# Flamingo block on one Trainium2 core: the recurrence of the fourth batch element, moved 4.8 places along the order of work

## The chip, the cores and the metric

The kernel runs on one core of a Trainium2 chip. The metric is the device time of one execution in microseconds (us), as the median of several runs. The engines are named as in the profile: PE is TensorE (matrix products and transposes; PEld is its weight load), DVE is VectorE, ACT is ScalarE, POOL is GpSimd, and SP issues nearly all DMAs. Each engine, and SP's queue, works through its own list of instructions in a fixed order.

## The reference

Four batch elements x[b] of 512 tokens by 512 channels pass through two layers, each an attention-like part and an FFN, all with residual sums and a gate (the tanh of a scalar):

```python
x = x + tanh(g_xattn[0]) * wkv(w, u, k=layernorm(x), v=ctx)          # "WKV"
x = x + tanh(g_ffn[0])   * ffn0(layernorm(x), w1, w2, w3)            # "FFN"
x = x + tanh(g_xattn[1]) * attention(layernorm(x), ctx, wq, wkv, wp) # "attention"
x = x + tanh(g_ffn[1])   * ffn1(layernorm(x), gamma, W)              # "ternary layer"
```

- **WKV** is a recurrence along the 512 tokens for every channel: a running maximum o, and two running sums p and q with decays; y = (A p + E v) / (A q + E), where A and E are exponentials of differences to the running maximum.
- **ffn0** is w3 of silu(w1 x) * (w2 x), with 2048 hidden channels, weights reduced to their sign times a mean, and activations rounded to 8 bits in groups of 64.
- **attention** has 16 heads of 32 channels; queries come from x (rounded to 8 bits), keys and values from the context ctx.
- **ffn1** normalises by the root mean square, rounds to 8 bits and multiplies with a weight matrix of -1, 0 and 1 times a scale.

The elements ("batch 0" to "batch 3" below, and their FFN stages by the same number) don't depend on one another. Inside one element the four parts follow each other.

## The kernel before

**Tiling.** Tokens are cut in NT = 4 tiles of 128, channels in NC = 4 chunks of 128, the FFN's hidden channels in NF = 4 quarters of 512. The first layer's FFN of one element has 16 *units*, one for each (token tile, quarter). A unit has two matrix products of 8 matmuls each (`up`, into the PSUM tile `ff_hp`; activations are split in two parts for precision), tanh on ACT (`gate`, L745), two products on DVE (L746, L750), rounding (`quantised`, L670-688, DVE, ACT, and POOL at L685), four transposes and a split (`parts`, L697 on DVE) and 8 matmuls into `ff_acc` (`down`).

**WKV of one element** is `wkv_layer(b, xb)`, from L562. It has three phases:

1. Statistics (`layernorm`, L191 and L194 on DVE, two small steps on POOL).
2. For each of the four token tiles: the normalised rows `wk_xn` on ACT (L215), four transposes into the PSUM tile `wk_ps` on PE, a copy to `wk_k` on ACT (L584).
3. For each of the four channel chunks, the generator `chunk(c)`: a scan for the running maximum (L599, DVE), a difference (L608, POOL), four Relu (L612) and two Exp (L614) on ACT, a scan for q (L629, DVE), products on POOL (L630, L635, L636, L641, L642) and DVE (L632, L645), a scan for p (L634, DVE), two reciprocals over 256 columns (L640, DVE), four transposes back (`wy_ps`), and the update of xb (L653, DVE). For b > 1, the context chunk `wk_v` comes from DRAM by a DMA (L594). A chunk has ten steps, and a chunk starts eight steps after the one before it (`in_steps(chains, 8)`).

The tiles of WKV come from a pool with one buffer each (`wk_k`, `wk_e`, `wk_o`, `wk_p`, `wk_q`, and `wk_v`, whose buffer `wk_xn` shares), so two elements' WKV can't be in flight together in the same phase.

**The order of work.** Four elements are in flight at different parts. Every part is a Python generator that issues a few instructions per step. `line(gen, (start, end, steps), ...)` registers a generator with a *place* for each step, spread evenly from start to end. `run` always takes the step with the smallest place. A place's whole number is a batch element's FFN: places b to b + 1 hold the 16 units of element b and one more, SLOTS = 17 places of the grid each (element 0's stage, with the weights' preparation, runs by its own scale up to 0.99). Below, "slot n of stage b" is b + n/17. So in stage 2, for example, lie:

- the FFN of element 2: slots 0 to 17.75
- the attention of element 0: its main part up to slot 5.95, its output projection to 8.35 (`project_out`, L1036, L1037 and others), its ternary layer from 8.95 to 13.95 (`ternary`: `tf_xn`, L219, L1147, L231, L1159, L1172)
- the attention of element 1: preparation at slots 1.7 to 4.35, the main part from 4.95 on (unit by unit: scores `s_ps`, maximum `at_nm` L948, Exp `at_P` L950, transposes `pt_ps` and copies `at_PT` L970, values `o_ps`)
- the WKV of element 3 (`next_batch(3)`)

Stage 1 holds the same for elements 1, 0 and 2, without the older element's tail, projection and ternary layer. Stage 3 holds the same as stage 2, one element on, without a WKV.

`next_batch(b)` is one step for the load of x[b] (L554), one for the statistics, four for the normalised rows and transposes (the last transposes come with the first chunk's step), and 32 for the chunks. This is the code that the change touches. On top of the issue order, the framework's scheduler decides the final place of each instruction on its engine, among those issued near it; so a step that is issued earlier stands earlier, but not by an exact count.

Of the kernel before, what the change touches and what calls it, by code (L numbers as in the profile page):

```python
# [30 lines left out]
def kernel(  # L31
# [1155 lines left out]
    def next_batch(b):  # L1187
        xs[b] = load_batch(b)
        yield
        yield from wkv_layer(b, xs[b])  # L1190
# [29 lines left out]
    SLOTS = NT * NF + 1  # L1220

    def line(gen, *parts, aside=False):
        lines.append({"gen": gen, "parts": parts, "step": 0, "aside": aside})

    xs = {}
    with (
# [19 lines left out]
        def at_unit(n):  # L1246
            return 0.3 + 0.67 * n / 16.0
# [84 lines left out]
            (at_unit(16), at_unit(16.4), 7),  # L1332
        )
        line(next_batch(1), (at_unit(0.5), at_unit(0.5), 1), (at_unit(0.6), at_unit(0.6), 1), (at_unit(2.0), at_unit(5.0), 4), (at_unit(5.0), at_unit(14.0), 32))
        for b in (2, 3):
            line(
                next_batch(b),
                (b - 1.0 - 4.2 / SLOTS, b - 1.0 - 4.2 / SLOTS, 1),
                (b - 1.0 - 3.2 / SLOTS, b - 1.0 - 3.2 / SLOTS, 1),
                (b - 1.0 + 1.8 / SLOTS, b - 1.0 + 5.8 / SLOTS, 4),  # L1340
                (b - 1.0 + 5.05 / SLOTS, b - 1.0 + 13.05 / SLOTS, 32),
            )
        run(0.99)
    nc.sync.dma_start(out=gamma_b, in_=bcast(gamma))
# [79 lines left out]
```

## Time and profile before

| what | value |
|---|---|
| runs | 1093.74, 1093.9, 1095.42 us; median 1093.9 us |
| the profiled execution | 1094.21 us; span of its instructions 1092.4 us, mean granted TensorE clock 0.956 |
| stage 1, first `ff_hp` product of unit 0 to that of stage 2 | 328.6 to 513.4 us |
| stage 2, the same way | 513.4 to 738.4 us |
| x[3] loaded by the DMA issued at | 279.4 us |
| WKV of element 3: statistics | 486.3 to 489.6 us (starts) |
| its copies to `wk_k` (L584) | 541.6, 555.7, 566.4, 570.5 us |
| its first scans (L599) | 571.2, 573.8, 605.2, 657.1 us |
| its updates of xb (L653) | 599.8, 636.7, 669.4, 697.0 us |
| statistics of element 3's FFN | 698.2 to 700.2 us (starts) |

A profile shows busy time of engines, and for each wait what ended it. Busy shares of the whole span are means over stages that differ; the windows (busy time of each engine in chosen stretches) show one stage at a time. [...]

### The profile page before, as it was taken

What the parts mean: (1) busy time and instruction counts of PE and PEld (TensorE: products, weight loads), DVE (VectorE), ACT (ScalarE), POOL (GpSimd) and SP (SyncE); (2) the same over time, 40 slices, a digit from 0 to 9 for tenths busy, and PEclk for the clock granted to TensorE, in tenths of its full rate; (3) what the DMA queues carried; (4) which work ended last, traced back from release to release, by engine and by line L of the source; (5) the groups of instructions that cost most, each with busy time, mean ns of one, the idle gap of its engine ahead of it and who ended that gap; (6) DMA issues with size and microseconds to landing.
All of it is one profiled execution on the core that took longest, in us unless ns stands there. A gap on an engine that the chain in (4) does not pass through costs nothing.

```text
span 1092.4 us, 17928 instructions
## 1 busy us (share of the span) xinstructions
PE 943.3 (86%) x6350; PEld 680.0 (62%) x6380; DVE 827.0 (76%) x1600; ACT 729.9 (67%) x1490; POOL 320.7 (29%) x328
## 2 busy tenths in 40 slices
PE   3879997998879888799997886999999999878975
PEld 2345564565557666677775665677776777655652
DVE  5985548757876899896769898966687866579976
ACT  5656755567545776667877576677685777877863
POOL 3831104423333254621215545412122410100000
PEclk8889999999999999999999798999999999989998
DMA  8188845464445674645576354655574563244311
GB/s 288 39 272 317 323 169 190 144 221 155 154 146 181 221 234 127 231 129 169 185 234 204 121 177 133 204 195 180 184 231 156 184 210 116 59 148 116 116 42 39
DMA packets 85674, 189.68 MB, mean 174 GB/s; under 512 B 12241, under 2 KB 36817, under 8 KB 74577
## 3 DMA queue, kind: packets, MB, share of 16 engines
q1 hardware_dynamic: 85584, 188.53, 51.7%
q8 instruction: 51, 0.84, 0.3%
q14 instruction: 39, 0.31, 0.1%
HBM read 148.65 MB, written 39.85 MB: 173 GB/s over the span
## 4 chain that ended last, share of the span: by engine, by line
PE 49%; DVE 22%; ACT 14%; POOL 5%; issue 5%; DMA 4%; SPq 1%; ACTq 0%; POOLq 0%; DVEq 0%
PE ff_hp L162 15%; PE pt_ps L165 7%; PE ff_acc L162 6%; PE o_ps L162 4%; PE v_ps L162 4%; PE s_ps L162 3%; ACT at_P L950 3%; DVE wk_q L640 3%; ACT at_PT L970 3%; DVE at_nm L948 2%; PE k_ps L162 2%; DVE wk_p L634 1%; PE qr_ps L165 1%; PE tp_ps L165 1%; ACT wk_e L612 1%
## 5 line engine op out<-in xcount | busy, mean ns | idle before, releaser
L162 PE MATMUL ff_hp<-wT,xp 128*128 128x512 f32 x1024 | 275.7, 412 | 6.6 <-DVE ff_z L746 3.7
L162 PEld LDWEIGHTS ff_hp<-wT,xp 128*128 128x128 f32 x1024 | 195.4, 196 | 54.6 <-DVE ff_z L746 5.7
L950 ACT ACTIVATE at_P<-s_ps,at_nm 128x512 f32<-128x512 f32 x256 | 175.0, 690 | 45.2 <-DVE at_nm L948 43.4
L948 DVE TENSOR_REDUCE at_nm<-s_ps 128x1 f32<-128x512 f32 x256 | 166.6, 677 | 38.4 <-PE s_ps L162 37.9
L970 ACT COPY at_PT<-pt_ps 128x512 f32<-128x512 f32 x224 | 131.2, 590 | 72.6 <-PE pt_ps L165 71.9
L685 POOL TENSOR_TENSOR ff_z<-qg_b,qg_s 128x512 f32<-128x512 bf16 x64 | 71.9, 1124 | 314.6 <-ACT qg_b L684 304.7
L165 PE MATMUL pt_ps<-ident,at_P 128*128 128x128 f32 x1024 | 155.4, 280 | 9.0 <-ACT at_PT L970 4.3
L165 PEld LDWEIGHTS pt_ps<-ident,at_P 128*128 128x128 f32 x1024 | 118.1, 142 | 47.3 <-ACT at_PT L970 10.9
L162 PE MATMUL ff_acc<-wT,hr 128*128 128x512 f32 x512 | 137.6, 409 | 5.2 <-DVE hr L697 2.6
L162 PE MATMUL s_ps<-at_kR,at_qR 128*128 128x512 f32 x256 | 103.0, 464 | 24.0 <-ACT at_P L950 17.6
L162 PEld LDWEIGHTS ff_acc<-wT,hr 128*128 128x128 f32 x512 | 92.9, 191 | 26.2 <-DVE hr L697 4.2
L162 PE MATMUL o_ps<-at_PT,at_V 128*32 128x128 f32 x2048 | 75.4, 281 | 4.7 <-ACT at_PT L970 2.8
L162 PEld LDWEIGHTS o_ps<-at_PT,at_V 128*32 128x32 f32 x2048 | 54.8, 111 | 28.6 <-issue 11.6
L746 DVE SCALAR_TENSOR_TENSOR ff_z<-ff_z,ff_hp 128x512 f32<-128x512 f32 x64 | 43.4, 679 | 37.0 <-ACT ff_z L745 36.9
L745 ACT ACTIVATE ff_z<-ff_hp,coef 128x512 f32<-128x512 f32 x64 | 44.1, 688 | 40.5 <-PE ff_hp L162 38.1
L750 DVE SCALAR_TENSOR_TENSOR ff_z<-ff_hp,coef,ff_z 128x512 f32<-128x512 f32 x64 | 47.7, 745 | 30.2 <-PE ff_hp L162 30.1
L684 ACT CAST qg_b<-qg_i 128x512 bf16<-128x512 int8 x80 | 49.3, 617 | 27.4 <-DVE qg_i L680 17.3
L162 PEld LDWEIGHTS s_ps<-at_kR,at_qR 128*128 128x128 f32 x256 | 43.3, 194 | 36.4 <-ACT at_P L950 25.2
L162 PE MATMUL v_ps<-wkvT,cT 128*128 128x512 f32 x128 | 60.5, 618 | 5.5 <-DVE wT L303 2.3
L162 PE MATMUL k_ps<-cT,wkvT 128*128 128x512 f32 x128 | 61.3, 631 | 2.3 <-ACT wk_k L584 1.0
L640 DVE RECIPROCAL wk_q<-wk_q 128x256 f32<-128x256 f32 x32 | 54.5, 1722 | 3.0 <-POOL wk_q L635 1.6
L696 ACT CAST hr<-tp_ps 128x512 fp32r<-128x512 f32 x64 | 37.6, 588 | 21.7 <-PE tp_ps L165 21.7
(180 smaller groups left out, 1669.4 us busy)
## 6 DMA issues: line engine op xcount, KB each, us to landing
wT<-wD SPq DMA_DIRECT2D x72, 1024.0 KB, 5.4
wn<-in_L_ffn_w_dram SPq DMA_DIRECT2D x18, 1024.0 KB, 6.2
at_kR<-kD SPq DMA_DIRECT2D x128, 128.0 KB, 4.0
at_qR<-qD SPq DMA_DIRECT2D x256, 64.0 KB, 2.5
wD<-wT SPq DMA_DIRECT2D x12, 1024.0 KB, 4.2
kD<-k_half SPq DMA_DIRECT2D x16, 512.0 KB, 2.8
qD<-at_half SPq DMA_DIRECT2D x32, 256.0 KB, 2.2
cn<-in_ctx_dram SPq DMA_DIRECT2D x8, 512.0 KB, 5.9
```

The costliest lines, as they stand in the source:

```text
L162: return in_turn(nc.tensor.matmul(*args, **kwargs))
L165: return in_turn(nc.tensor.transpose(*args))
L640: nc.vector.reciprocal(half, half)
L684: nc.scalar.copy(qb, qi)
L685: nc.gpsimd.tensor_tensor(grouped(src), grouped(qb), s.unsqueeze(2).to_broadcast([P, NG, GS]), ALU.mult)
L696: nc.scalar.copy(part[:, 0, :], pt)
L745: nc.scalar.activation(z, hp, AF.Tanh, scale=coef[:, 0:1])
L746: nc.vector.scalar_tensor_tensor(z, z, 1.0, hp, ALU.add, ALU.mult)
L750: nc.vector.scalar_tensor_tensor(z, hp, coef[:, 1:2], z, ALU.mult, ALU.mult)
L948: nc.vector.tensor_reduce(nm, sp, AX.X, ALU.max, negate=True)
L950: nc.scalar.activation(lanes[k, i, t], sp, AF.Exp, bias=nm, accum_out=sums[k][:, t, i : i + 1],)
L970: made[k] = nc.scalar.copy(dst, blocks(pt))
```

## The change

The registration of `next_batch(b)` for b = 2 and b = 3 is rewritten around a helper `slot(n)`, with a shift `first` that is 0 for element 2 and -4.8 slots for element 3.

| step | element 2 before | element 2 after | element 3 before | element 3 after |
|---|---|---|---|---|
| load | slot -4.2 of stage 1 | -4.2 | slot -4.2 of stage 2 | -9.0 |
| statistics | -3.2 | -2.8 | -3.2 | -7.4 |
| rows and transposes (4 steps) | 1.8 to 5.8 | 1.8 to 4.6 | 1.8 to 5.8 | -3.0 to -0.2 |
| chunks (32 steps) | 5.05 to 13.05 | 5.05 to 13.05 | 5.05 to 13.05 | 0.25 to 8.25 |

Negative slots lie in the stage before: slot -7.4 of stage 2 is slot 9.6 of stage 1, and -3.0 is 14.0. What the steps compute is the same.

```diff
-        for b in (2, 3):
+        for b, first in ((2, 0.0), (3, -4.8)):
+
+            def slot(n, b=b, first=first):
+                return b - 1.0 + (first + n) / SLOTS
+
             line(
                 next_batch(b),
-                (b - 1.0 - 4.2 / SLOTS, b - 1.0 - 4.2 / SLOTS, 1),
-                (b - 1.0 - 3.2 / SLOTS, b - 1.0 - 3.2 / SLOTS, 1),
-                (b - 1.0 + 1.8 / SLOTS, b - 1.0 + 5.8 / SLOTS, 4),
-                (b - 1.0 + 5.05 / SLOTS, b - 1.0 + 13.05 / SLOTS, 32),
+                (slot(-4.2), slot(-4.2), 1),
+                (slot(-3.2 + 0.2 * b), slot(-3.2 + 0.2 * b), 1),
+                (slot(1.8), slot(4.6), 4),
+                (slot(5.05), slot(13.05), 32),
             )
```

## The prediction

> **What bounds the kernel now.** I read the page first (busy shares and the 40 slices), then the windows of each engine cut at the FFN units, then the groups of VectorE (DVE) with the waits in the stretch where the two disagree. A "unit" is one of the 16 (token tile, FF quarter) pairs of a batch's FFN, numbered from 0. It is cut where its first DVE gating instruction (L746) starts, read from the timeline.
>
> The page alone would say TensorE:
>
> ```profile
> PE 943.3 (86%) x6350; PEld 680.0 (62%) x6380; DVE 827.0 (76%) x1600; ACT 729.9 (67%) x1490; POOL 320.7 (29%) x328
> ```
>
> The windows say that this is an average over two kinds of stage. Columns: stretch, length, busy us (instructions) of each engine, TensorE's granted clock, DMA share, GB/s. In order, the rows are: batch 1 units 5-12, units 13-15; batch 2 units 0-4, 5-7, 8-13, 14-15; batch 3 units 0-7, 8-13.
>
> ```profile
> core 0: us, PE busy (x) PEld busy (x) DVE busy (x) ACT busy (x) POOL busy (x), PEclk, DMA share, GB/s
> 369.60:472.40 102.80, 87.23 (x602) 67.11 (x606) 97.08 (x152) 71.18 (x149) 50.76 (x50) 0.95 0.56 182
> 472.40:516.30 43.90, 41.13 (x354) 32.05 (x342) 35.00 (x84) 34.46 (x79) 9.65 (x10) 1.00 0.54 168
> 516.30:570.10 53.80, 52.58 (x426) 41.87 (x423) 36.73 (x84) 40.38 (x87) 11.21 (x12) 1.00 0.61 207
> 570.10:624.00 53.90, 42.18 (x251) 30.04 (x246) 47.47 (x75) 36.48 (x70) 30.01 (x28) 0.87 0.56 185
> 624.00:711.60 87.60, 73.52 (x553) 57.32 (x547) 77.43 (x158) 59.06 (x122) 40.69 (x40) 0.94 0.51 168
> 711.60:741.40 29.80, 28.33 (x235) 22.00 (x233) 19.96 (x43) 23.03 (x54) 4.05 (x4) 1.00 0.54 180
> 741.40:828.90 87.50, 85.44 (x655) 66.97 (x652) 66.72 (x152) 63.48 (x138) 20.93 (x20) 1.00 0.65 208
> 828.90:901.40 72.50, 69.45 (x524) 53.75 (x527) 51.27 (x119) 49.77 (x110) 21.00 (x22) 0.98 0.52 171
> ```
>
> Where WKV chunks run (369.6-472.4 and 570.1-711.6), DVE is 88 to 94% busy, TensorE 78 to 85%, and the clock sags. Where they don't, TensorE is 94 to 98% busy and DVE 67 to 80%. Batch 3 has the same work as batch 2 in the same units except WKV (the older batch's attention tail, its projection, its ternary layer, the younger batch's attention), so it is the row for "batch 2 without WKV". Units 5-13: 53.9 + 87.6 = 141.5 us in batch 2, and 901.4 - 793.4 = 108.0 us in batch 3 (its unit 5 starts at 793.4). The fourth element's WKV costs 33.5 us where it stands.
>
> What it brings to DVE there (count | busy, mean ns):
>
> ```profile
> L640 DVE RECIPROCAL wk_q<-wk_q 128x256 f32<-128x256 f32 x8 | 13.5, 1719 | 0.5 <-POOL wk_q L635 0.5
> L634 DVE TENSOR_TENSOR_SCAN wk_p<-wk_e 128x512 f32<-128x512 f32 x4 | 6.3, 1564 | 0.5 <-POOL wk_e L630 0.5
> L629 DVE TENSOR_TENSOR_SCAN wk_q<-wk_e 128x512 f32<-128x512 f32 x4 | 5.1, 1286 | 1.9 <-ACT wk_e L614 1.9
> L599 DVE TENSOR_TENSOR_SCAN wk_o<-wc,wk_k 128x512 f32<-128x512 f32 x4 | 4.9, 1214 | 1.5 <-POOL wk_p L608 1.4
> L632 DVE TENSOR_TENSOR wk_q<-wk_e,wk_q 128x512 f32<-128x512 f32 x4 | 4.3, 1080 | 0.0
> L645 DVE TENSOR_TENSOR wk_e<-wk_e,wk_q 128x512 f32<-128x512 f32 x4 | 3.5, 877 | 0.0
> L653 DVE SCALAR_TENSOR_TENSOR xb<-wy_ps,gates,xb 128x512 f32<-128x512 f32 x4 | 3.0, 742 | 0.8 <-PE wy_ps L165 0.8
> ```
>
> That is 40.6 us in 32 instructions. Records of neighbours overlap by some 0.08 us (two at_nm reductions of 0.68 stand as 1.27), so it takes about 38 us of DVE.
>
> The waits of 570-712 name what TensorE loses there: the old batch's ternary layer, late because DVE and POOL are busy with WKV.
>
> ```profile
> PE qr_ps L165 <- ACT tf_xn L231: 8.6, 1, 8.6
> ```
>
> **The change, part by part.** I set the two built instruction orders beside each other, cut at the same units. On DVE the chunks' first scans (L599) go from batch 2 units 5, 5, 7, 10 to units 0, 0, 2, 3, and the last xb update (L653) from unit 12 to unit 8; so the change does what its words say. Summing each moved instruction's median duration in the trace, DVE's records in units 0-4 rise from 42.4 to 65.6 us, in 5-7 they stay at 49.8 (one part of WKV replaces another), and in 8-13 they fall from 87.5 to 64.4. No instruction is added or removed.
>
> *Batch 2, units 0-7.* Now 53.8 + 53.9 = 107.7 us. After: DVE has batch 3's 66.7 us of these units plus WKV's 38 = 104.4 to 104.7 us, against 85.4 us of TensorE; DVE becomes the bound. How full can it be? 97.08/102.8 = 94% in batch 1's WKV stage, 47.47/53.9 = 88% in units 5-7, where WKV meets the attention projection. At 94%: 110.7 us, so **+3.0 us**. Ends: full DVE, 104.5 (-3.2); 88%, 118.8 (+11.1). I take 94%, since most of the stretch is WKV beside FFN and attention, as in batch 1; only units 6-8 have the projection. The cover that TensorE gave in units 0-4 (17 us of free DVE) is used up by this: nothing more can be hidden there.
>
> *Batch 2, units 8-13.* Now 87.6 us. Without WKV it is batch 3's 72.5 us. The FFN's own statistics of xb3 (four L191 of 0.67 plus small ones, about 3.4 us of DVE) now fall in units 8-10 and not in unit 13, and a last L653 (0.74) in unit 8; DVE then has 51.3 + 4 of 72.5 us, so they lie under TensorE. The other end: this stretch's own TensorE time of 73.5 us (at a clock of 0.94) at batch 3's 69.45/72.5 fill gives 76.7. So -15.1 to -10.9; I take **-14**, near the row with the same content. The 8.6 us stall goes; what ends last there next is TensorE's own queue, as in batch 3. Units 14-15 (29.8 us) don't move: TensorE is 95% busy.
>
> *Batch 1.* The four first statistics of xb3 (L191, 0.67 each, and four L194: 3.4 us) move from units 13-14 to units 9 and 11, inside batch 1's DVE-bound stage. There they cost up to 3.4; where they leave, TensorE (41.1 of 43.9) hides them, and later statistics may ride on a wait: **+2**, ends 0 and 3.4. The normalised rows and transposes of b = 3 (four L215 of 0.82 and four L584 of 0.59 on ACT, four groups of four transposes at 0.66 on TensorE) go from units 2-5 of batch 2 to units 12-15 of batch 1 and unit 0. TensorE bounds units 13-15, so three groups, 2.0 us, are on the path; ACT's 5.1 us fits (34.5 of 43.9 busy), unless a copy is late: **+2**, ends 0 and 4. For b = 2, one L215 and one L584 stand one unit earlier (4 to 3) and its statistics a little later; units 0-4 are TensorE's (33.3 of 35.4 us busy by the same cut): 0, ends ±0.5.
>
> *Queues.* SP: the x load of b = 3 stands at the same place of SP's queue (it already ran at 279.4). Four wk_v loads (L594) move ahead with the chunks; each waits for POOL's L636 of the chunk before, 11.1 us in three waits at 500-720, the longest 4.7, and wT, at_kR and at_qR loads queue behind them. No idle of TensorE in 500-720 is ended by a DMA, so I put 0 on it; without that cover, one wait of 4.7 us is the price. POOL: some 30 us of WKV products move with the chunks; units 0-4 have 11.2 of 53.8 busy, and its ff_z products (1.04 each) then queue behind products of 1.3 to 2.3 us. That is inside the 94%.
>
> Two rules of the Trainium skill stand beside these rows. The first: L632 took 0.68 to 1.78 us over the run and L634 1.21 to 2.29. "SBUF — State Buffer", section "Who interferes with whom", has a DVE instruction with two SBUF inputs and a GpSimd one block each other for a whole instruction. By it, leaving the ternary layer's POOL work behind would shorten them, by 0.76 us a chunk at most (1080 to 677 and 1564 to 1210 ns), an estimate of 3 us on the sum, 1084. But batch 1's chunks, with no ternary layer beside them, have means of 1333 and 1557 ns; by that row it is nothing, and I book nothing. The second speaks against the change: "Perfetto Trace Analysis", section "Identifying the Most-Contended Engine", says to work on the engine with the highest occupancy first, with a caveat for TensorE. By the page's 86% that is TensorE, whose work doesn't shrink, and the sum would be 0; the windows show that DVE is fuller in exactly the 141 us at issue.
>
> **Sum.** +3.0 - 14 + 2 + 2 = -7.0 us; ends -3.2 - 15.1 - 0.5 = -18.8 and 11.1 - 10.9 + 3.4 + 4 + 0.5 = +8.1 (with the SP wait +12.8). The profiled execution took 1094.2 us (span 1092.4), 0.3 over the median of 1093.9. So **1087** us. 0.2% (2.2 us) is about what a measurement of this kernel can tell from no change.
>
> **Rivals.**
> - *Slower: a chunk keeps its price wherever it stands.* The 33.5 us are then chain and queue, not crowding: units 0-7 take 87.5 + 33.5 = 121 us, +13.3; with -14 and +4 that is +3.3, 1097. For it: units 5-7 lose 11 us of TensorE time with DVE at only 88%, and half of that stretch's collision (chunks beside the projection, L1036 and at_o) exists after the change as well. Against: batch 1's four chunks ran at 94%. It decides once four chunks cost over 30.2 + 2.2 us in units 0-7 (mine: 23.2).
> - *No change.* The same sum between: 28 to 32 us for the chunks there, 1092 to 1096. Total DVE and TensorE work is the same, and one DVE-bound stretch replaces another; for it speaks that the sum of the fuller engine by part hardly moves, against it the 8.6 us wait, which has a named cause that leaves.
> - *Faster than forecast.* DVE runs full in units 0-7 and batch 1 hides its 4 us: -3.2 - 15 + 1 = -17, 1077. For it: unit 6 of batch 2 was 100% DVE. Against: ACT's exponentials and POOL's products stand between DVE's steps.
>
> **How the numbers follow.** Forecast (1082 to 1091.5) 0.42, faster still 0.18, no change 0.15, slower 0.25. So faster 0.60, within 0.2% 0.15, slower 0.25. The forecast's range is 1082 to 1091.5; with one in ten left out on each side it is 1079 to 1098.
>
> **What would show it.** Right: the last xb3 update near unit 8 (some 70 us earlier); units 0-7 of batch 2 near 111 us with DVE at 94%; units 8-13 near 73.5 with a clock near 0.98 and no tf_xn wait of several us; units 9-15 of batch 1 some 4 us longer; batch 3 unchanged. Wrong: units 0-7 over 118 us, or new idle of TensorE in them ended by at_qR or wT loads, or units 8-13 still above 80, which would mean that the ternary layer stalls by itself.

## The result, and the profile after

The kernel after takes 1100.5 us (median; 1100.4 to 1101.9 in four runs), the kernel before 1094.1 us on the same chip. The ratio is 1.0059 with a 95% interval of 1.0045 to 1.0073: **slower by 0.6%**. The prediction was 1087 us with a range of 1079 to 1098, so the sign and the range are wrong.

The page's first line hardly differs from the one before: the same work is done.

```profile
PE 943.8 (86%) x6380; PEld 677.7 (62%) x6380; DVE 826.2 (75%) x1600; ACT 729.3 (66%) x1490; POOL 320.2 (29%) x328
```

The windows of the kernel after, cut at the same DVE instruction (L746) as those before. The columns are the stretch, its length, busy us (instructions) of each engine, TensorE's granted clock, DMA share and GB/s. The rows are: batch 1 units 5-12 and 13-15; batch 2 units 0-4, 5-7, 8-13, 14-15; batch 3 units 0-7 and 8-13; and last, batch 2 units 0-7 as one stretch.

```profile
core 0: us, PE busy (x) PEld busy (x) DVE busy (x) ACT busy (x) POOL busy (x), PEclk, DMA share, GB/s
371.10:477.70 106.60, 87.80 (x601) 66.81 (x604) 100.16 (x163) 71.45 (x150) 52.33 (x52) 0.95 0.56 176
477.70:522.40 44.70, 41.85 (x364) 32.97 (x354) 32.21 (x75) 37.24 (x84) 7.89 (x8) 1.00 0.55 177
522.40:594.40 72.00, 58.95 (x435) 44.72 (x428) 60.70 (x100) 49.83 (x100) 32.94 (x34) 0.95 0.52 163
594.40:643.10 48.70, 39.12 (x242) 29.73 (x241) 44.43 (x81) 31.31 (x64) 25.25 (x21) 0.89 0.54 184
643.10:718.00 74.90, 69.51 (x535) 53.62 (x533) 55.40 (x138) 50.50 (x109) 23.32 (x25) 1.00 0.52 168
718.00:747.80 29.80, 28.33 (x235) 21.96 (x233) 19.98 (x43) 23.03 (x54) 4.06 (x4) 1.00 0.54 176
747.80:835.60 87.80, 85.87 (x657) 66.86 (x651) 66.54 (x152) 63.54 (x138) 20.98 (x20) 1.00 0.67 230
835.60:908.20 72.60, 68.35 (x528) 52.74 (x527) 51.27 (x120) 49.83 (x110) 21.04 (x22) 1.00 0.53 171
522.40:643.10 120.70, 98.07 (x675) 74.45 (x668) 105.13 (x179) 81.14 (x163) 58.19 (x54) 0.93 0.53 171
```

The profiled execution of after took 1101.9 us, 1.4 above its median; the medians differ by 6.4 us. Where the 7.7 us between the two profiled spans (1092.4 and 1100.1) come from:

| stretch | before | after | difference | forecast |
|---|---|---|---|---|
| up to batch 1 unit 0 | 334.2 | 335.5 | +1.3 | 0 |
| batch 1 units 0-4 | 35.4 | 35.6 | +0.2 | 0 |
| batch 1 units 5-15 | 146.7 | 151.3 | +4.6 | +4 |
| batch 2 units 0-7 | 107.7 | 120.7 | **+13.0** | **+3.0** |
| batch 2 units 8-13 | 87.6 | 74.9 | -12.7 | -14 |
| batch 2 units 14-15 | 29.8 | 29.8 | 0 | 0 |
| batch 3 units 0-13 | 160.0 | 160.4 | +0.4 | 0 |
| the rest | 191.0 | 191.9 | +0.9 | 0 |

One term fails. Units 0-7 lose as much as units 8-13 gain. VectorE (DVE) is busy there for 105.1 us, within 0.6 us of the 104.5 that were worked out for it. But it idles for 15.6 us, so it is 87% full; at 94% it would idle for 6.2. The groups of DVE in units 0-7 (count | busy, mean ns | idle time before them and what ended it) show how much of this idle time stands at the chunks' own steps:

```profile
L640 DVE RECIPROCAL wk_q<-wk_q 128x256 f32<-128x256 f32 x8 | 13.8, 1734 | 1.1 <-POOL wk_q L635 1.1
L634 DVE TENSOR_TENSOR_SCAN wk_p<-wk_e 128x512 f32<-128x512 f32 x4 | 8.1, 2025 | 1.7 <-POOL wk_e L630 1.7
L746 DVE SCALAR_TENSOR_TENSOR ff_z<-ff_z,ff_hp 128x512 f32<-128x512 f32 x9 | 6.0, 668 | 2.1 <-ACT ff_z L745 2.1
L750 DVE SCALAR_TENSOR_TENSOR ff_z<-ff_hp,coef,ff_z 128x512 f32<-128x512 f32 x8 | 5.7, 716 | 3.1 <-PE ff_hp L162 3.1
L629 DVE TENSOR_TENSOR_SCAN wk_q<-wk_e 128x512 f32<-128x512 f32 x4 | 5.2, 1305 | 2.9 <-ACT wk_e L614 2.9
L599 DVE TENSOR_TENSOR_SCAN wk_o<-wc,wk_k 128x512 f32<-128x512 f32 x4 | 4.9, 1218 | 2.3 <-ACT wk_k L584 1.3 <-POOL wk_p L608 1.1
L645 DVE TENSOR_TENSOR wk_e<-wk_e,wk_q 128x512 f32<-128x512 f32 x4 | 3.8, 954 | 1.5 <-POOL wk_e L642 1.5
```

Summed over the chunk's lines (with 0.9 us at L653) this is 10.5 us of DVE idle time directly ahead of chunk steps. In batch 1's WKV stage before, from which the 94% was taken, the same sum is 1.7 us. The waits are short, up to 1.5 us each, and nearly all are ended by ACT or POOL. Another 3.6 us stand at the FFN's gating steps L746 and L750 (of the 2.1 us at L746, 1.5 lie ahead of the stretch's first instruction).

The good half of the change came as foreseen. TensorE's waits from 600 us on hold no `tf_xn` any more; the longest is this, inside units 5-7:

```profile
PE qr_ps L165 <- ACT at_o L231: 4.5, 1, 4.5
```

### The profile page after: what moved, and what is told of

It is laid out like the page before. It is cut to its first block, busy times and chain, and to the rows that moved or that the text cites. A ratio compares the mean times of both kernels' runs of the same rounds, so it can differ in the third digit from the quotient of the medians.

```text
span 1100.1 us, 17966 instructions
## 1 busy us (share of the span) xinstructions
PE 943.8 (86%) x6380; PEld 677.7 (62%) x6380; DVE 826.2 (75%) x1600; ACT 729.3 (66%) x1490; POOL 320.2 (29%) x328
## 4 chain that ended last, share of the span: by engine, by line
PE 45%; DVE 24%; ACT 15%; POOL 7%; issue 5%; DMA 3%; SPq 1%; ACTq 0%; POOLq 0%; DVEq 0%
PE ff_hp L162 14%; PE pt_ps L165 7%; PE ff_acc L162 6%; PE o_ps L162 4%; ACT at_P L950 3%; PE s_ps L162 3%; PE v_ps L162 3%; DVE at_nm L948 3%; DVE wk_q L640 2%; ACT at_PT L970 2%; PE k_ps L162 2%; DVE wk_p L634 2%; ACT wk_e L612 2%; DVE ff_z L750 1%; DVE wk_q L629 1%
## 5 line engine op out<-in xcount | busy, mean ns | idle before, releaser
L162 PE MATMUL ff_hp<-wT,xp 128*128 128x512 f32 x1024 | 276.4, 413 | 15.9 <-DVE ff_z L746 12.8
L948 DVE TENSOR_REDUCE at_nm<-s_ps 128x1 f32<-128x512 f32 x256 | 166.8, 678 | 39.1 <-PE s_ps L162 39.0
L685 POOL TENSOR_TENSOR ff_z<-qg_b,qg_s 128x512 f32<-128x512 bf16 x64 | 71.3, 1114 | 320.0 <-ACT qg_b L684 309.7
L750 DVE SCALAR_TENSOR_TENSOR ff_z<-ff_hp,coef,ff_z 128x512 f32<-128x512 f32 x64 | 47.5, 742 | 32.4 <-PE ff_hp L162 32.4
L746 DVE SCALAR_TENSOR_TENSOR ff_z<-ff_z,ff_hp 128x512 f32<-128x512 f32 x64 | 43.5, 679 | 33.8 <-ACT ff_z L745 33.5
L640 DVE RECIPROCAL wk_q<-wk_q 128x256 f32<-128x256 f32 x32 | 54.6, 1724 | 2.6 <-POOL wk_p L628 1.4
L950 ACT ACTIVATION_READ_ACCUMULATOR at_P<-s_ps,at_nm 128x1 f32 x256 | 52.3, 204 | 0.0
```

The lines of the kernel that those rows point to most:

```text
L162: return in_turn(nc.tensor.matmul(*args, **kwargs))
L640: nc.vector.reciprocal(half, half)
L685: nc.gpsimd.tensor_tensor(grouped(src), grouped(qb), s.unsqueeze(2).to_broadcast([P, NG, GS]), ALU.mult)
L746: nc.vector.scalar_tensor_tensor(z, z, 1.0, hp, ALU.add, ALU.mult)
L750: nc.vector.scalar_tensor_tensor(z, hp, coef[:, 1:2], z, ALU.mult, ALU.mult)
L948: nc.vector.tensor_reduce(nm, sp, AX.X, ALU.max, negate=True)
```

## The experiments

Edits are to the kernel after unless another is named. "Units 0-7" are batch 2's. "Chunk idle" is DVE's idle time directly ahead of WKV's steps in the stretch named. Ratios are to the kernel before. Unit times come from one profiled execution each, so they stand for a run and not for a median. How far one such time can be trusted shows in batch 1's units 5-12, where no_recip and later_scan (below) have the same instructions in the same order on DVE, ACT and POOL. They took 104.0 us at a granted clock of 0.97 in the one profile and 108.4 us at 0.92 in the other:

```profile
372.87:476.84 103.97, 86.67 (x602) 66.14 (x606) 100.86 (x162) 71.45 (x150) 52.20 (x52) 0.97 0.57 181
370.76:479.17 108.41, 90.21 (x598) 68.81 (x604) 100.58 (x163) 71.42 (x150) 52.42 (x52) 0.92 0.54 172
```

So a difference of some 4 us in one long stretch isn't by itself the effect of an edit.

### Which part of the change costs

**rows_early**: element 3's statistics and rows move, its chunks stay where they were. Element 2 is as in after.

```diff
-                (slot(5.05), slot(13.05), 32),
+                (b - 1.0 + 5.05 / SLOTS, b - 1.0 + 13.05 / SLOTS, 32),
```

> Element 3's load, statistics, rows and transposes stand as in the changed kernel (slots -9.0, -7.4 and -3.0 to -0.2), its chunks as in the kernel before (5.05 to 13.05). Theory P (a chunk keeps its price wherever it stands, some 8.4 us for each of the four): the gain from units 8-13 never comes, the loss in units 0-7 neither, and only batch 1's cost is left: units 9-15 of batch 1 take 113 us from unit 8 on as in the changed kernel (108.4 before), less up to 2 us for the transposes that leave units 2-5 of batch 2; time 1096 to 1099. Rival S (batch 1's cost comes from the chunks of element 3 already pressing on its last units): batch 1 as before, time 1092 to 1094.

1098.5 us, ratio 1.0041 (1.0026 to 1.0057). Batch 1 loses 5.6 us from unit 5 on, units 0-7 take 104.4 us, units 8-13 take 88.9. So the statistics and rows, with element 2's small moves, cost 4 us, and the chunks' move adds only about 2 more, which is the balance of +16 in units 0-7 and -14 in units 8-13. The forecast for that move was -11.

**no_shift**: no shift of element 3. What is left of the change are steps of a fraction of a slot (statistics later by 0.4 for element 2 and by 0.6 for element 3, rows closed up).

```diff
-        for b, first in ((2, 0.0), (3, -4.8)):
+        for b, first in ((2, 0.0), (3, 0.0)):
```

> The rewrite with a shift of 0 for element 3 as well: only the later statistics and the tighter rows of elements 2 and 3 are left (statistics at -2.8 and -2.6, rows and transposes from 1.8 to 4.6, chunks where they were). If the cost of the change lies in the shift, this is within 1.5 us of the kernel before: 1093 to 1095.5. If the small moves cost by themselves (batch 0's unit 12 took 1.3 us longer in the changed kernel, where element 2's statistics stand), 1096 or more.

1098.1 us, ratio 1.0043 (1.0027 to 1.0059). For element 2 moves of this size had been costed at 0, at most 0.5 us, and those of both elements cost 4: unit 12 of batch 0 takes 18.7 us and not 17.2, batch 1's units 13-15 take 47.8 and not 43.9 (the profiled run, 1102.2 us, was the longest of ten).

**rows_only**: the kernel before with element 3's rows alone moved (its statistics and chunks stay).

```diff
-                (b - 1.0 + 1.8 / SLOTS, b - 1.0 + 5.8 / SLOTS, 4),
+                (b - 1.0 + 1.8 / SLOTS, b - 1.0 + 5.8 / SLOTS, 4)
+                if b == 2
+                else (b - 1.0 - 3.0 / SLOTS, b - 1.0 - 0.2 / SLOTS, 4),
```

> The kernel before with one part of the change alone: element 3's rows and transposes stand at slots -3.0 to -0.2, its statistics, its chunks and all of element 2 where they were. Batch 1's cost in the changed kernel (4.6 us) is split by it. If the statistics in batch 1's VectorE-bound units 9 and 11 make it, batch 1 costs 2 us or less here, batch 2 gains the 3.3 us that its units 0-7 gained with the early rows, and the time is 1091 to 1094. If the transposes on the full TensorE make it, batch 1 costs 4 us or more and the time is 1094 to 1097.

1097.6 us, ratio 1.0034 (1.0022 to 1.0046). Batch 1's units 13-15, where TensorE was 41.1 of 43.9 us busy, grow by 4.7 us: the early rows and transposes cost more there than the 2.0 us that the transposes themselves take. The costs of the parts don't add up: by the medians no_shift alone costs 3.7 us and rows_only 3.1, while rows_early, with both kinds of move, costs 4.1.

### What a chunk costs, and whether work or crowding sets it

**no_wkv2**: the kernel before without the chunks of element 2 in batch 1's stage (their work is left out).

```diff
+        def idle(c):
+            for _ in range(10):
+                yield True
+
-        chains = [chunk(c) for c in range(NC)]
+        chains = [(idle if b == 2 else chunk)(c) for c in range(NC)]
```

> The kernel before with the chunks of element 2 left out (its rows and transposes stay; element 2's WKV is not added). It measures what four chunks cost in batch 1, where no older attention, projection or ternary layer runs beside them. If the price is the same everywhere (theory P), units 5-13 of batch 1 shorten by 30 us or more, time 1060 to 1065. If it is lower where less other work stands (the 94% of VectorE that the forecast took from there is a lower price), by 16 to 24 us, time 1070 to 1078.

1066.4 us, ratio 0.975 (0.9728 to 0.9772). Units 5-12 of batch 1 take 80.1 us, against 102.8 with the chunks:

```profile
369.00:449.10 80.10, 79.36 (x609) 63.16 (x610) 61.77 (x136) 58.05 (x131) 15.51 (x17) 1.00 0.68 220
```

That is 22.7 us less, but the chunks' last update (473.0 us) lies in unit 13. Over units 5-13, the units of the 33.5 us in batch 2, the difference is 26.9 us (117.3 against 90.4), and over the whole kernel 28.1 (1066.4 against 1094.5). Stretch and time both fall between the ranges of the two theories. So four chunks cost 33.5 us in batch 2 before, 33.2 there after (120.7 less batch 3's 87.5) and 27 to 28 in batch 1. That speaks against the rival "a chunk keeps its price wherever it stands", but not decisively by itself, and the price in batch 1 isn't the 23.2 us that the forecast had for units 0-7.

**spread**: the chunks begin as in after and end as in before.

```diff
-                (slot(5.05), slot(13.05), 32),
+                (slot(5.05), b - 1.0 + 13.05 / SLOTS, 32),
```

> As the changed kernel, but element 3's 32 chunk steps are spread from slot 0.25 to 13.05, not to 8.25. The same instructions, at 5/8 of the density. Theory D (what costs is crowding: VectorE is the bound only while chunk work and the rest exceed it, 104 us of VectorE against 85 us of TensorE in units 0-7): at lower density units 0-7 have some 91 us of VectorE and units 8-13 some 69, so units 0-13 of batch 2 take 172 to 182 us in place of 195.6; time 1080 to 1090. Theory P (a chunk's own chain of steps stalls the in-order queues, 8.4 us a chunk at any density): units 0-13 stay at 193 to 197 us, time 1099 to 1102.

1099.6 us, ratio 1.0052 (1.0037 to 1.0067). Units 0-13 take 191.7 us; in after they take 195.6, before 195.3. Batch 3's same units, without WKV, take 160.0. So over a third less density (12.8 slots for 8) wins 4 us of some 35: crowding is not the main thing. The stretch lies between the ranges of both theories, nearer to P, and the median gains 0.9 us.

**no_bias**: two bias additions of POOL beside the chunks are left out (L874, the last two tiles of batch 1).

```diff
-            nc.gpsimd.tensor_tensor(xb[:, t, :], xb[:, t, :], bp_b, ALU.add)
+            if b != 1 or t < 2:
+                nc.gpsimd.tensor_tensor(xb[:, t, :], xb[:, t, :], bp_b, ALU.add)
```

> The changed kernel with the two additions of the output bias to element 1's last two token tiles left out (L874 on POOL, 1.28 us each, at 541.1 and 544.9 us of the changed kernel's profile, between two steps of the first chunk), so that part of the result lacks the bias. Theory Q (the new place collides with the preparation of element 1's attention on POOL: the chunk's products wait behind its POOL work, and VectorE behind those): units 0-3 of batch 2 take 3 us or more less, 1095 to 1098. Theory D (VectorE is simply full): 2.6 us of POOL matter only by the blocking of VectorE's two-input steps, under 1.5 us: 1099 to 1101.

1102.3 us, ratio 1.0075 (1.0058 to 1.0093): no faster. Units 0-7 take 119.8 us, with a chunk idle of 7.9. The time lies above the ranges of both theories. DVE's instructions stand in the same order as in after, so this is a clean test of these two neighbours, and they aren't the price.

**no_pool**: two of POOL's five products in each chunk of element 3 are left out (L630, L642).

```diff
-            nc.gpsimd.tensor_tensor(E2, E2, v, ALU.mult)
+            if b < 3:
+                nc.gpsimd.tensor_tensor(E2, E2, v, ALU.mult)
...
-            nc.gpsimd.tensor_tensor(A, A, E, ALU.add)
+            if b < 3:
+                nc.gpsimd.tensor_tensor(A, A, E, ALU.add)
```

> The changed kernel with two of element 3's five POOL products per chunk left out (L630, on which VectorE's scan L634 waits, and L642, on which its product L645 waits; some 2.9 us of POOL a chunk), so the values of the recurrence are wrong for element 3. VectorE's work stays. Theory V: units 0-7 of batch 2 shorten by under 4 us (POOL's blocking of VectorE's two-input steps), time 1096 to 1101. Theory C: two steps of each chunk's chain go, 2 us or more a chunk, units 0-7 shorten by 8 us or more, time under 1093.

1100.0 us, ratio 1.0056 (1.0035 to 1.0076). Units 0-7 take 116.2 us: 4.5 less, between the bounds of the two theories. DVE's busy time accounts for 4.0 of it (105.1 to 101.1), its idle time for 0.5. So a shorter chain through POOL did not make DVE wait less in sum. The waits for L630 and L642 went, and that at the reciprocal rose from 1.1 to 4.1 us. The 4.5 us don't show in the median, which is 0.5 us below that of after.

**no_recip**: the eight reciprocals of element 3 are left out (L640), 13.8 us of DVE.

```diff
-                nc.vector.reciprocal(half, half)
+                if b < 3:
+                    nc.vector.reciprocal(half, half)
```

> The changed kernel with element 3's eight reciprocals left out (L640, 1.72 us each, 13.8 us of VectorE), so element 3's WKV is not divided by its denominator. In units 0-7 of batch 2 the chunks cost 33.2 us (120.7 against 87.5 without WKV in batch 3). Theory V (the time that the chunks take of VectorE lies on the path nearly whole, because the FFN and the attention keep too few buffers to wait out a chunk's burst): units 0-7 shorten by 11 to 14 us, time 1086 to 1090. Theory C (the wait along the chunk's steps over POOL and ScalarE sets the price, and VectorE stands idle within it): they shorten by 3 to 7 us, time 1093 to 1098.

1115.6 us, ratio 1.0198 (1.017 to 1.0225): **15 us slower than after**, with less work. Units 0-7 take 133.4 us. Two timelines of this kernel (start us, us, engine, line, operation; idle time before it and what ended it) show a piece of how. Its lines from 641 on stand one higher than in the kernel after. DVE:

```profile
540.37 1.26 DVE L222 TENSOR_REDUCE at_s<-at_xn 128x1 f32<-128x512 f32 x2
546.54 1.74 DVE L646 TENSOR_TENSOR wk_e<-wk_e,wk_q 128x512 f32<-128x512 f32 x1 [4.91 <-POOL wk_e L643]
548.20 0.74 DVE L751 SCALAR_TENSOR_TENSOR ff_z<-ff_hp,coef,ff_z 128x512 f32<-128x512 f32 x1
```

and POOL, which works through all of this time:

```profile
538.15 2.18 POOL L635 TENSOR_TENSOR wk_q<-wk_q,wk_e 128x512 f32<-128x512 f32 x1
540.29 1.28 POOL L875 TENSOR_TENSOR xb<-xb,bp_b 128x512 f32<-128x512 f32 x1
541.54 1.27 POOL L636 TENSOR_TENSOR wk_e<-wk_e,wk_v 128x512 f32<-128x512 f32 x1
542.78 1.26 POOL L642 TENSOR_TENSOR wk_e<-wk_e,wk_p 128x512 f32<-128x512 f32 x1
544.02 1.27 POOL L875 TENSOR_TENSOR xb<-xb,bp_b 128x512 f32<-128x512 f32 x1
545.25 1.25 POOL L643 TENSOR_TENSOR wk_e<-wk_e 128x512 f32<-128x512 f32 x1
```

With the reciprocals gone, the product L646 came up at DVE while POOL still had some 5 us of work ahead of what it needs. DVE stood for 4.91 us, and the FFN's gating step L751, which is next in its queue, stood behind it. TensorE had finished what L751 reads at 543.4 us, and its next `ff_hp` product then waited for L751:

```profile
539.90 3.51 PE L162 MATMUL ff_hp<-wT,xp 128*128 128x512 f32 x8 [4.13 <-DVE ff_z L747]
548.99 2.56 PE L162 MATMUL ff_hp<-wT,xp 128*128 128x512 f32 x8 [3.39 <-DVE ff_z L751]
```

But the reciprocals aren't all that changed. The scheduler, left with less work on DVE, also placed some of DVE's other steps differently (36 of 170 in units 0-7): in after the same gating step (L750) stands ahead of the chunk's product (L645), not behind it. DVE of the kernel after:

```profile
544.50 0.65 DVE L750 SCALAR_TENSOR_TENSOR ff_z<-ff_hp,coef,ff_z 128x512 f32<-128x512 f32 x1
547.43 1.75 DVE L645 TENSOR_TENSOR wk_e<-wk_e,wk_q 128x512 f32<-128x512 f32 x1 [1.48 <-POOL wk_e L642]
```

So the run shows what a wait at the wrong place costs. How much of the 15 us is the missing cover of the reciprocals, and how much the new order, isn't separated. Over units 0-7 DVE waited 10.7 us at L646. DVE's busy time fell by only 6 us, to 99.2, since others grew: L646 from 0.95 to 1.74 us, for one.

The Trainium skill, "Perfetto Trace Analysis", section "Identifying the Most-Contended Engine", says to optimise the engine with the highest occupancy first. DVE is that engine in units 0-7 (87%), and taking work off it, with the order that came of it, made the stretch 12.7 us longer. The page's next section, "Optimization Strategy", says to look for the gaps on that engine and for what ends them, which is what this timeline needed.

**later_scan**: each chunk of element 3 gets one more step between its exponentials and its first sum, and the chunks stand nine steps apart.

```diff
+            if b == 3:
+                yield True
             A, E2, E, A2 =
...
-            yield from in_steps(chains, 8)
+            yield from in_steps(chains, 9 if b == 3 else 8)
...
-                (slot(5.05), slot(13.05), 32),
+                (slot(5.05), slot(13.05 if b == 2 else 14.05), 32 if b == 2 else 36),
```

> The changed kernel with one more step per chunk of element 3, an empty one between its exponentials and its scan for q, so that VectorE's and POOL's steps of the chunk stand later than the steps they wait for (chunks start nine steps apart, 36 steps from slot 0.25 to 9.25). Theory W (the price is VectorE standing still in its fixed order: in the changed kernel it idles 15.5 us in units 0-7 of batch 2, 10.5 us of that directly ahead of steps of the chunks, against 5.4 and 1.7 in batch 1's WKV stage): the idle ahead of chunk steps falls to 6 us or less and the time by 3 to 6 us, to 1095 to 1098. Rival R (idle moves to the other steps, because the whole loop of TensorE, VectorE and ScalarE is closed): the idle of VectorE in the chunks' stretch stays within 2 us of 15.5 and the time within 2 us of 1100.5.

1098.8 us, ratio 1.0039 (1.0024 to 1.0054). The chunk idle falls from 10.5 to 4.5 us, and the stretch hardly shortens (119.2 us): DVE now waits at the FFN's gating steps, 4.4 us at L746 for ACT and 2.8 at L750 for TensorE. Idle time at the chunk's steps is thus not by itself what is lost. Without it, DVE waits elsewhere.

### Where the chunks begin

**shift8** and **shift53** shift all of element 3's steps by another amount:

```diff
-        for b, first in ((2, 0.0), (3, -4.8)):
+        for b, first in ((2, 0.0), (3, -8.0)):
```

> The changed kernel with a shift of -8.0 slots instead of -4.8 for element 3: statistics at slot 6.4 of stage 1, rows from 10.8 to 13.6, chunks from 14.05 of stage 1 to 5.05 of stage 2, clear of the older element's projection, but over the preparation of element 1's attention. Theory P (a chunk costs 8.3 us at any place of stage 2): 1098 to 1102. Theory N (the price follows the other elements' POOL and ScalarE steps beside the chunk: 5.7 us a chunk in batch 1 where there are none of preparation, projection or ternary layer): two chunks meet less of them, 1092 to 1097.

1106.2 us, ratio 1.0093 (1.0065 to 1.012). Units 0-7 fall to 103.0 us, but batch 1's units 13-15, which now hold the first chunk, rise to 61.1.

```diff
-        for b, first in ((2, 0.0), (3, -4.8)):
+        for b, first in ((2, 0.0), (3, -5.3)):
```

> The changed kernel with a shift of -5.3 slots instead of -4.8: half a unit earlier, so that the chunks' steps meet other steps of the FFN's unit. If the price depends on how the chunk's steps fall between the steps of a unit, this differs from 1100.5 by 3 us or more, to either side; theory P says 1099 to 1102.

1095.3 us, ratio 1.0007 (0.9995 to 1.0019): half a slot takes 5 us off, although batch 1's units 5-12, where the statistics go, take 110.4 us in this profile (after: 106.6). Units 0-7:

```profile
528.00:638.90 110.90, 93.14 (x653) 70.08 (x656) 104.13 (x177) 79.37 (x163) 57.07 (x52) 0.95 0.56 189
```

That is the forecast stretch: 110.7 us at 94%. Set against the last row of the windows of after, DVE's busy time differs by 1 us and the length by 9.8.

**start_m025**, **start_005**, **start_075** move the chunks alone, to begin at -0.25, 0.05 and 0.75 (after: 0.25), with rows and statistics as in after.

```diff
-                (slot(5.05), slot(13.05), 32),
+                (slot(5.05), slot(13.05), 32)
+                if b == 2
+                else (b - 1.0 + -0.25 / SLOTS, b - 1.0 + (-0.25 + 8.0) / SLOTS, 32),
```

> The changed kernel, only element 3's chunks start at slot -0.25 and not at 0.25 (to 7.75); rows, statistics and element 2 as in the changed kernel. Theory F (phase within the unit sets VectorE's idle): units 0-7 of batch 2 take 109 to 113 us as with the shift of -5.3 (110.9; 120.7 in the changed kernel), batch 1 as in the changed kernel, time 1090 to 1093. Rival G (the good run came from its earlier rows and statistics, which left batch 1's part longer): 117 us or more, time over 1097.

1094.6 us, ratio 1.0004 (0.9992 to 1.0016). Units 0-7 as foreseen, the whole 1.6 us above the range given:

```profile
523.10:635.00 111.90, 93.17 (x653) 69.83 (x656) 103.59 (x178) 79.31 (x163) 57.11 (x52) 0.95 0.54 179
```

> The changed kernel, only element 3's chunks start at slot 0.75 (to 8.75): the phase of -0.25, one unit later. Units 0-13 of batch 2 take 195.7 us in the changed kernel and 183.3 with the shift of -5.3. Theory F: 183 to 187, time 1090 to 1094. Theory A (the absolute place beside preparation, projection and the rest decides): 191 or more, time over 1096.

1105.7 us, ratio 1.0102 (1.0075 to 1.0129). Units 0-13 take 200.1 us, 4.5 more than in after. That the price repeats from unit to unit (theory F: 183 to 187) falls.

> The changed kernel, only element 3's chunks start at slot 0.05 (to 8.05), just after the FFN's steps as in the kernel before (5.05) and not level with the step after. Theory F: between the two phases, units 0-13 of batch 2 at 185 to 194 us, time 1091 to 1099. It says how wide the good phase is.

1095.5 us, ratio 1.0016 (1.0005 to 1.0026), units 0-13 187.7 us.

**start_m025_two**: start_m025, and element 2's statistics and rows where they were before the change.

```diff
-                (slot(-3.2 + 0.2 * b), slot(-3.2 + 0.2 * b), 1),
-                (slot(1.8), slot(4.6), 4),
+                (slot(-3.2 + 0.6 * (b - 2)), slot(-3.2 + 0.6 * (b - 2)), 1),
+                (slot(1.8), slot(5.8 if b == 2 else 4.6), 4),
```

> As start_m025, with element 2's statistics and rows left where the kernel before has them. In the changed kernel batch 0's unit 12 is 1.3 us longer, where element 2's statistics stand; if that is their cost, this is 1 to 2 us faster than start_m025 (1088.5 to 1092), and the fastest of all versions here. Otherwise equal to it within 1 us.

1091.6 us, ratio 0.9975 (0.9964 to 0.9985): **faster than both kernels**. Against start_m025, element 2's moves of a fraction of a slot are worth 3.0 us. Units 0-7:

```profile
521.00:634.10 113.10, 95.68 (x653) 72.14 (x656) 104.54 (x178) 79.16 (x163) 57.22 (x52) 0.92 0.54 178
```

### Is it the neighbour in POOL's queue?

At -0.25 and at 0.25 POOL's queue differs most in one place (a few of the FFN's own products, L685, stand elsewhere too, and DVE's list differs at many places). In after, the attention preparation of batch 1's last two tiles (L219, L874) stands between the products of chunk 0. POOL of the kernel after, and DVE's product that waits for it:

```profile
533.96 2.42 POOL L219 TENSOR_SCALAR at_xn<-xb,ln_r 128x512 f32<-128x512 f32 x2
536.35 1.69 POOL L630 TENSOR_TENSOR wk_e<-wk_e,wk_v 128x512 f32<-128x512 f32 x1
...
541.14 1.28 POOL L874 TENSOR_TENSOR xb<-xb,bp_b 128x512 f32<-128x512 f32 x1
...
544.86 1.29 POOL L874 TENSOR_TENSOR xb<-xb,bp_b 128x512 f32<-128x512 f32 x1
546.10 1.30 POOL L642 TENSOR_TENSOR wk_e<-wk_e 128x512 f32<-128x512 f32 x1
547.34 1.29 POOL L608 TENSOR_TENSOR wk_p<-wk_k,wk_o 128x512 f32<-128x512 f32 x1
```

DVE of the kernel after, where L645 waits for that L642:

```profile
547.43 1.75 DVE L645 TENSOR_TENSOR wk_e<-wk_e,wk_q 128x512 f32<-128x512 f32 x1 [1.48 <-POOL wk_e L642]
```

In start_m025 the products come first and the preparation after them. POOL of start_m025:

```profile
536.66 1.29 POOL L642 TENSOR_TENSOR wk_e<-wk_e 128x512 f32<-128x512 f32 x1
546.08 1.53 POOL L219 TENSOR_SCALAR at_xn<-xb,ln_r 128x512 f32<-128x512 f32 x2
```

and DVE of start_m025, where the same product doesn't wait:

```profile
541.00 0.67 DVE L645 TENSOR_TENSOR wk_e<-wk_e,wk_q 128x512 f32<-128x512 f32 x1
```

Two experiments registered that preparation alone at another place. The scheduler then moved other instructions as well: in prep_before POOL's remaining list in units 0-7 is that of after, but 21 of DVE's 143 other instructions stand elsewhere; so do 21 of DVE's 142 in prep_among, set against start_m025. **prep_before** (edit to after) puts it ahead of chunk 0's products; **prep_among** (edit to start_m025, with 0.3 for 0.5) puts it between them, in the sequence of after.

```diff
+        prep = 0.5 if b == 1 else 1.7
...
-            (b + 1 + 1.7 / SLOTS, b + 1 + 3.7 / SLOTS, 5),
-            (b + 1 + 3.75 / SLOTS, b + 1 + 4.35 / SLOTS, 2),
+            (b + 1 + prep / SLOTS, b + 1 + (prep + 2.0) / SLOTS, 5),
+            (b + 1 + (prep + 2.05) / SLOTS, b + 1 + (prep + 2.65) / SLOTS, 2),
```

> The kernel after, with the attention preparation of batch 1's last two tiles (L219 and L874 on GpSimd, the rows' transposes) registered 1.2 slots sooner, from slot 0.5 of stage 2 and not 1.7; element 3's chunks start at 0.25 as in after. In GpSimd's order the preparation then stands ahead of chunk 0's products (L630 to L642) and not between them. Theory N (the neighbour on GpSimd's queue sets the chunks' waits): units 0-7 of batch 2 take 110 to 115 us (after 120.7), VectorE's idle time ahead of chunk steps falls from 10.5 us to 6 or less; time 1093 to 1097. Theory A (the place of the chunks against all else decides, whatever stands between the products): units 0-7 stay at 118 to 122 us, time 1099 to 1102.

1106.1 us, ratio 1.0103 (1.0082 to 1.0124); units 0-7 take 124.1 us, chunk idle 7.1. Neither theory: worse than both.

> Start_m025 (element 3's chunks from slot -0.25, 1094.6 us, units 0-7 111.9), with the same attention preparation of batch 1 registered from slot 0.3 and not 1.7. In GpSimd's order L219 and L874 then stand between chunk 0's products, in the same sequence as in the kernel after. Theory N: units 0-7 rise to 116 to 121 us, idle time of VectorE ahead of chunk steps from 4.9 us to 8 or more; time 1098 to 1102. Theory A: units 0-7 stay at 110 to 114 us, time 1093 to 1096.

1109.6 us, ratio 1.014 (1.0124 to 1.0155); chunk idle 6.3. Units 0-7, and DVE's groups at the FFN's gating steps:

```profile
524.20:652.40 128.20, 98.70 (x657) 74.39 (x656) 105.03 (x178) 80.44 (x163) 57.06 (x52) 0.87 0.49 157
L746 DVE SCALAR_TENSOR_TENSOR ff_z<-ff_z,ff_hp 128x512 f32<-128x512 f32 x9 | 6.0, 671 | 6.2 <-ACT ff_z L745 6.2
L750 DVE SCALAR_TENSOR_TENSOR ff_z<-ff_hp,coef,ff_z 128x512 f32<-128x512 f32 x8 | 5.8, 722 | 5.5 <-PE ff_hp L162 5.3
```

The price moves as the neighbour theory says, by twice as much, but not at the place that it names: what grew are DVE's waits at the FFN's L746 (to 6.2 us) and L750 (to 5.5), more than those at the chunk's steps (4.9 to 6.3). Since the swap failed in prep_before, and leaving out L874 (no_bias) won nothing, the neighbour on POOL's queue isn't the cause by itself.

**start_m075_two**: start_m025_two with the chunks from -0.75 (both -0.25 replaced by -0.75).

> Start_m025_two (1091.6 us: element 2 as before the change, element 3's chunks from slot -0.25, units 0-7 113.1), with element 3's chunks from slot -0.75. Theory A (an earlier start costs less on and on): units 0-7 at 108 to 111 us, units 13-15 of batch 1 some 2 us longer than its 46.7, time 1087 to 1090.5. Theory N (chunk 0's products are ahead of the preparation already, nothing more to win): units 0-7 at 111 to 115 us, time 1090.5 to 1095.

1100.0 us, ratio 1.0057 (1.0035 to 1.0078). Batch 1's units 13-15 rise from 46.7 to 55.4 us, and units 0-7 stay at 113.9. An earlier start doesn't gain on and on: what leaves units 0-7 is paid with more in batch 1.

### What stands after the experiments

Batch 1's units 13-15 and batch 2's units 0-7 together, with nearly the same work in each. The two columns of idle time are DVE's in units 0-7: directly ahead of chunk steps, and directly ahead of the FFN's gating steps and the attention's maximum (L746, L750, L948), which wait for TensorE's products or for ACT's step on them:

| kernel | chunks from slot | the two stretches, us | DVE busy in units 0-7, us | idle, chunk steps | idle, gates and maximum | time, us |
|---|---|---|---|---|---|---|
| shift8 | -2.95 | 61.1 + 103.0 = 164.1 | 89.8 | 2.6 | 6.6 | 1106.2 |
| start_m075_two | -0.75 | 55.4 + 113.9 = 169.3 | 98.8 | 3.9 | 5.4 | 1100.0 |
| start_m025_two | -0.25 | 46.7 + 113.1 = 159.8 | 104.5 | 4.6 | 0.8 | 1091.6 |
| start_m025 | -0.25 | 46.7 + 111.9 = 158.6 | 103.6 | 4.9 | 1.0 | 1094.6 |
| shift53 | -0.25 | 47.2 + 110.9 = 158.1 | 104.1 | 4.2 | 0.2 | 1095.3 |
| start_005 | 0.05 | 44.7 + 114.5 = 159.2 | 103.6 | 6.4 | 3.3 | 1095.5 |
| after | 0.25 | 44.7 + 120.7 = 165.4 | 105.1 | 10.5 | 3.6 | 1100.5 |
| start_075 | 0.75 | 44.7 + 124.5 = 169.2 | 108.1 | 1.7 | 8.5 | 1105.7 |
| prep_before | 0.25 | 44.7 + 124.1 = 168.8 | 104.8 | 7.1 | 10.7 | 1106.1 |
| prep_among | -0.25 | 46.7 + 128.1 = 174.8 | 105.0 | 6.3 | 12.7 | 1109.6 |

Shown: with the chunks inside units 0-7 and 103.6 to 105.1 us of DVE work there, units 0-7 take 111 to 121 us according to half a slot of the chunks' start, and up to 128 when the attention's preparation is moved too. What varies is DVE's waiting. Between start_m025 and after it differs by 7.3 us, and 5.6 more stand at the chunk steps. In the three longest (prep_among, start_075, prep_before) it stands more at the gates and the maximum; start_075 waits least of all at the chunk steps, 1.7 us. The granted clock alone doesn't make the difference: start_m025_two takes 113.1 us at 0.92, after 120.7 at 0.93. How much of prep_among's 128.1 us goes with its clock of 0.87 isn't shown.

Open is which pair of neighbours makes an arrangement good. The price is neither a property of the chunk, nor of the crowding, nor of POOL's queue at one place, and no rule of place that I tried (a fraction of the unit, earlier is better) held.

## Why the prediction was wrong

- **What bounds the kernel, and that the change does what it says: right.** DVE's busy time in units 0-7 came out at 105.1 us (104.5 forecast); the last xb update falls in unit 8, at 644.2 us, 53 us earlier (some 70 forecast; 10 of the missing 17 are units 0-7's own growth beyond the forecast).
- **"At 94%: 110.7 us, so +3.0 us": the step that failed.** The fill was 87% (15.6 us of DVE idle and not 6.2), and the term is +13.0 us, beyond its own range's 88% (+11.1). The step took a busy share from one stage and carried it to another. shift53 and start_m025 show that 110.9 and 111.9 us are there to be had with the same work half a slot earlier, so the 94% wasn't impossible. But nothing in the trace of before bore on whether this order would reach it, and the row that did combine WKV with the projection, units 5-7, had 88%.
- **"Units 8-13, -14": right**, -12.7. The `tf_xn` stall is gone, the clock is 1.00 (near 0.98 foreseen), and TensorE is the fuller engine again.
- **Batch 1, +2 and +2: right in sum (+4.6), by luck in part.** In after units 5-12, where element 3's statistics go, carry +3.8, and units 13-15 +0.8. In rows_only, where the statistics stay, the rows cost 4.7 us in units 13-15. So each part seems to have cost about twice its forecast, and the statistics' leaving, booked at nothing, to have given some 4 us back. The +3.8 isn't sharp: start_m025_two, with the same statistics of element 3, has +1.2 in its profile, and two profiles of the same order there differ by 4.4.
- **"For b = 2 ... 0, ends ±0.5": too small.** Unit 12 of batch 0 grew by 1.3 us in after and is back at 17.2 us in start_m025_two, and element 2's moves are worth 3.0 us by that run (1091.6 against 1094.6).
- **Queues, 0: held as far as DMA goes.** No wait among the longest in units 0-7 is ended by a DMA. That POOL's products would be "inside the 94%" was not so: 5.4 us of the chunk idle are ended by a product of POOL.
- **The slower rival had the stretch's number (121 us; its 1097 us for the whole was too low), not the mechanism.** By its own sign, over 32.4 us for four chunks in units 0-7, it came true with 33.2. But the 33.5 us are no fixed price: half a slot earlier the chunks cost 24.4 us there (start_m025: 111.9 less 87.5) and 2.0 more in batch 1's units 13-15, and in batch 1 four cost 26.9 (no_wkv2).
- **The estimate by the page on SBUF.** By the Trainium skill's "SBUF — State Buffer", section "Who interferes with whom", the sum was an estimated 1084 us for the move away from the ternary layer's POOL work, by shorter L632 and L634. Measured, L632 did shorten (1080 to 932 ns), but L634 lengthened (1564 to 2025 ns). The rule itself is in line with no_pool: with two POOL products fewer a chunk, L634 takes 1506 ns and L632 765.

## What to carry to other kernels

A busy share is a result of one order of work. When steps move to another stage, an engine's work there can be added up (here within 1%), but its waits can't. The worst fill that the trace of before showed for such a mixture, 88%, was near the outcome here, but it is no bound either: with the same DVE work the orders tried gave 82% (prep_among) to 94% (shift53). Where queues are in order, try a move at several offsets of a fraction of a place before judging it, and keep small moves of other steps apart from it: here half a slot was worth 5 us and a few tenths of a slot for another element 3 us, of the size of the move's own loss (6 us).

## What the runs showed of the hardware

- An instruction that waits holds up what is ready behind it: in no_recip DVE stood 4.91 us at L646, while what L751 reads was finished at 543.4 us. L751 ran at 548.20, and TensorE's next `ff_hp` product waited 3.39 us for it. That kernel had 13.8 us less work on the fullest engine and was 15 us slower, in an order that the scheduler had changed too.
- One DVE product of 128x512 (L645) took 1.75 us while POOL was running L608 and 0.67 us while POOL did nothing (after at 547.43, start_m025 at 541.00); two single instructions.
- The same order can run at different granted clocks: 104.0 us at 0.97 (no_recip) and 108.4 us at 0.92 (later_scan) for batch 1's units 5-12, with the same DVE, ACT and POOL lists. In units 0-7 the clock was 0.95 in start_m025, 0.93 in after and 0.87 in prep_among. Whether a lower clock makes waits or waits lower the clock, no run shows.
